# Layer 0's expert routing: all tiles at once behind the last norm, or four tiles at a time behind each group's norm

## The chip, the cores and the metric

The kernel runs on one core of one Trainium2 chip. The metric is the device time of one execution in microseconds (us); lower is better. Three runs of the kernel before took 4592.47, 4594.38 and 4607.38 us, so the median is 4594.38.

The engines are named as the profile names them: PE (TensorE, matrix products; PEld is its loading of weights), DVE (VectorE), ACT (ScalarE), POOL (GpSimd, which here issues the gathers and scatters whose rows are picked by an index) and SP (SyncE, which here issues plain copies).

## What is computed

Four layers of a graph network over 3125 nodes with 256 features and 50000 edges. Each layer adds a graph convolution and a mixer to x, then a feed-forward part with experts. The change touches layer 0 alone:

```python
xn = _layernorm(x)
x = x + _L0_gnn_ref(xn, src, dst, edge_type, ...) + _L0_mix_ref(xn, ...)
x = x + _L0_ffn_ref(_layernorm(x), ...)

# _L0_ffn_ref: each token goes to one of 8 experts, which take at most C = 489 tokens
probs = softmax(x @ gate_w + gate_b)
idx = argmax(probs)                      # the token's expert
prb = probs[idx]
one_hot = one_hot(idx, 8)
pos = (cumsum(one_hot, axis=0) * one_hot).sum(-1) - 1    # its place in the expert's list
kept = pos < C
buf = zeros(8, C, 256).at[idx, where(kept, pos, C)].set(x, mode='drop')
ybuf = relu(buf @ w1 + b1) @ w2 + b2     # per expert
y = ybuf[idx, minimum(pos, C - 1)] * (prb * kept)
```

The place pos is a running count over all tokens, so a token's row in buf depends on all tokens ahead of it, and on none behind it.

## The kernel before

The nodes lie in 25 tiles of 128 (T = 25, P = 128), which are handled in groups of four (GROUPS: six groups of four tiles and one of a single tile). The method fast() writes the whole run.

**Layer 0's first half** (lines 2384 to 2403) is a drive() of four generators that take turns: in each round seg_near makes three steps, l0_mix one, norm_after one, and sort_places two.
- seg_near (L434) is the graph convolution. The edges are sorted by destination and lie in 391 chunks of 128. Step i issues gather i on POOL (L447): 128 rows of a table in DRAM, picked by gi, go to one of 16 buffers G. The same step works off chunk i - 12: a one-hot of the destinations is made on DVE (L416) and multiplied on PE (L430, tile seg). When the last chunk of a tile is done, close (l0_close, L1027) adds the result to x and puts the tile on the list closed. Tile t closes with chunk 16t + 18.
- l0_mix (L1046) is the mixer. It puts a tile on the list mixed when it has been added to x.
- norm_after (L186) waits until the four tiles of a group are on both lists. Then it normalises them (norm_tiles, L170 to L181: statistics at L174 and L175, xn at L178, transposes on PE at L165) and calls then(t0, n), which before is gate0: sixteen small products with the gate's weights and an addition, which gives the group's scores pr (L1117).
- sort_places (L620) works out rows for a later sort of the edges by source.

**Behind the drive** the first 16 scatters of send (L687, table by_src) are issued on POOL. Then l0_ffn (L1121) does the experts. It clears the table moe_buf in DRAM with two copies from zeros (L1128 and L1130), takes the softmax of all 25 tiles' scores at once (L263 to L270), finds the first maximum (first_max, L219, with an iota made on POOL at L254), counts with two products against a triangle and against ones (L1140, L1142), sums over the tiles with one scan (L1151), and gets the rows wi for writing and ri for reading. Then 25 scatters on POOL (L357) send the tiles of xn to moe_buf. Eight experts follow: their rows are loaded (L1183), transposed (L1188) and multiplied. While they run, a Pump lets one by_src scatter of POOL go after every 700 columns of product. At the end 25 gathers on POOL (L351, yt) fetch each token's result, and the next norm follows.

**What sets the order.** A scheduling layer orders the instructions of PE, DVE, ACT and SP within a region when the program is built. POOL's are kept as the code issues them (manual_schedule for Pool around fast()). Each engine then works off its list, and semaphores make it wait for other engines' results. All plain copies of this part go through SP's queue.

Of the kernel before, what the change touches and what calls it, by code (L numbers as in the profile page):

```python
# [7 lines left out]
F32 = mybir.dt.float32  # L8
BF16 = mybir.dt.bfloat16
I32 = mybir.dt.int32  # L10
AF = mybir.ActivationFunctionType
OP = mybir.AluOpType
AX = mybir.AxisListType
# [4 lines left out]
P = 128  # L18
N = 3125
T = 25  # L20
NP = T * P
TAIL = N - (T - 1) * P
D = 256
# [11 lines left out]
CAP = 489  # L35
# [29 lines left out]
def drive(*gens):  # L65

    live = list(gens)
    while live:
        for g in list(live):
            for _ in range(g[1]):  # L70
                try:
                    next(g[0])
                except StopIteration:
                    live.remove(g)
                    break
# [19 lines left out]
class Net:  # L95
# [1022 lines left out]
                                 gb[:, None, :].to_broadcast([P, n, 8]))  # L1118
        return pr, gate

    def l0_ffn(self, pool, lean=False, pr=None):  # L1121
        nc, a = self.nc, self.a
        NE, FF = 8, 1024
        full = [P, T, NE]
        buf = self.dram.tile([NE * CAP, D], F32, name="moe_buf")
        ybuf = self.dram.tile([NE * CAP, D], F32, name="moe_y")
        flat = bass.AP(tensor=buf.tensor, offset=buf.offset, ap=[[NE * CAP * D // P, P], [D, 30], [1, D]])
        nc.sync.dma_start(flat, self.zeros[:, None, :].to_broadcast([P, 30, D]))  # L1128
        rest = NE * CAP * D // P - 30 * D
        nc.sync.dma_start(bass.AP(tensor=buf.tensor, offset=buf.offset + 30 * D,  # L1130
                                  ap=[[NE * CAP * D // P, P], [1, rest]]), self.zeros[:, :rest])
        if pr is None:
            pr, gate = self.l0_gate(pool)
            gate(0, T)
        self.softmax_last(pool, pr, full, "pr")
        iota = self.iota_e(pool, T, NE, "l0r")
        oh, prob, idx = self.first_max(pool, pr, full, iota, "l0r")
# [14 lines left out]
        pre = pool.tile(full, F32, name="pre")  # L1152
        nc.vector.tensor_add(pre, cum.rearrange("p e t -> p t e"), before.rearrange("p (t e) -> p t e", e=NE))
        nc.vector.tensor_mul(pre, pre, oh)
        pos = pool.tile([P, T], F32, name="pos")
# [3 lines left out]
        slot = pool.tile([P, T], F32, name="slot")  # L1159
        wi = pool.tile([P, T], I32, name="wi")  # L1160
        ri = pool.tile([P, T], I32, name="ri")
# [5 lines left out]
        nc.vector.tensor_mul(prob, prob, kept)  # L1167
        for t in range(T):
            self.scatter_apart(buf.name, buf, wi[:, t:t + 1], self.xn[:, t, :])
        inf = pool.tile([P, 4 * NE], F32, name="inf")  # L1170
        nc.vector.memset(inf, 0.0)
        b1 = self.load(pool, "b1", a["L0_ffn_b1"])
        mt = [(i * P, min(P, CAP - i * P)) for i in range(4)]
        for e in range(NE):
# [10 lines left out]
            for k in range(2):  # L1185
                p = self.ps(CAP)
# [4 lines left out]
            for f in range(FF // P):  # L1191
                p = self.ps(CAP)
# [3 lines left out]
            for i, (m0, m) in enumerate(mt):  # L1196
                p = self.ps(D, parts=m)
# [17 lines left out]
        p = self.ps(1)  # L1215
        nc.tensor.matmul(p, self.ones, fin, start=True, stop=True)
        nc.vector.tensor_scalar(ok, p, P - 0.5, None, op0=OP.is_gt)
        with self.tc.If(self.value(ok) > 0) as branch:
            for t0, n in GROUPS:
                for t in range(t0, t0 + n):  # L1220
                    y = self.gather(pool, "yt", ybuf, ri[:, t:t + 1], D, 4)
                    nc.vector.scalar_tensor_tensor(self.x[:, t, :], y, prob[:, t:t + 1], self.x[:, t, :],
                                                   op0=OP.mult, op1=OP.add)
# [1145 lines left out]
    def fast(self):  # L2369

        nc, tc, a = self.nc, self.tc, self.a
        g = self.g
        with tc.tile_pool(name="keepf", bufs=1) as keep, tc.tile_pool(name="dramf", bufs=1, space=DRAM) as dram:
# [7 lines left out]
            self.deg2 = keep.tile([P, T], F32, name="deg2")  # L2381
            ok4 = keep.tile([P, 1], I32, name="ok4")
            self.beyond = keep.tile([P, 1], F32, name="beyond")
            pr0, gate0 = self.l0_gate(keep)
            order = tp("order")
            op = order.__enter__()
            place = op.tile([P, C1], I32, name="place")
            rec = op.tile([P, C1, 3], F32, name="rec")
            with tp("gl0") as gp, Banks(self, **sums):
                gi = gp.tile([P, C1], I32, name="gi")  # L2390
                closed = set()
                with tp("set0") as sp:
                    ty = self.load(sp, "type", a["type"], dtype=I32)
                    nc.vector.scalar_tensor_tensor(gi, g["src"], 4.0, ty, op0=OP.mult, op1=OP.add)
                    nc.scalar.copy(rec[:, :, 2], self.load(sp, "weight", a["weight"]))
                    dst = self.load(sp, "dst", a["dst"], dtype=I32)
                    nc.scalar.copy(rec[:, :, 0], dst)
                    nc.scalar.copy(rec[:, :, 1], g["src"])
                with tp("mix0") as mp, tp("sort0") as sp:
                    skey = self.bits(sp, g["src"], "skey", 7)  # L2400
                    drive((self.seg_near(gp, g, self.h_tab, gi, self.l0_close(gp, closed), True), 3),
                          (self.l0_mix(mp), 1), (self.norm_after(closed, self.mixed, then=gate0), 1),
                          (self.sort_places(sp, skey, C1, T, self.sbase, place, 40), 2))
            with Banks(self, **plain):
                sorted_e = dram.tile([P * C1, 3], F32, name="by_src")
                send = self.send(sorted_e, place, rec, C1)
                for _ in range(16):
                    next(send)
                with tp("ffn0") as p:
                    self.pump = Pump(tc, send, 700)  # L2410
                    for _ in self.l0_ffn(p, True, pr0):
                        pass


            with tp("att1") as gp:
                closed, self.mixed = set(), set()
                pre = gp.tile([P, 4 * EG, 4], F32, name="pre")
# [353 lines left out]
```

## Time and profile before

| | us |
|---|---|
| median of three runs | 4594.38 |
| the profiled execution: its time | 4595.59 |
| its span on the core | 4593.9 |
| first gather of layer 0, last gather of layer 0 (start) | 147.2, 659.7 |
| scores of the seven groups, pr (start) | 420.7, 433.2, 451.0, 511.9, 591.8, 667.1, 685.0 |
| 25 scatters to moe_buf (start of the first and of the last) | 694.9, 725.8 |
| first load of the experts' rows, first product on them | 728.4, 730.4 |
| last gather of the experts' results (start) | 1008.6 |

The busiest engines over the span are PE with 3624.3 us and POOL with 2627.7. The profile is of one execution; a row of the timeline gives start and length in us, the engine, the line of the kernel, the operation, what it writes and reads, how many there are, and in brackets how long the engine was idle before it and what it waited for. The clock given is the one that PE was granted.

### The profile page before, as it was taken

Reading aid. Unit: us, or ns where it says so; the run is one execution under the profiler, and the core shown is the slowest. Engines: PE = TensorE matmul, PEld = TensorE weight load, DVE = VectorE, ACT = ScalarE, POOL = GpSimd, SP = SyncE. Lnnn points to the kernel's source line nnn. Section 1 sums busy time; section 2 is a strip of 40 time slices with the busy share of each in tenths; the row PEclk is TensorE's granted clock in tenths of the full one; section 3 lists DMA queues with packets and bytes.
Section 4 is the critical chain, followed back from the end, with each engine's and each line's share of the span. In section 5 each row is a group of like instructions: output and inputs, shape, how many; then the busy total and the mean of one; then the engine's idle time right before and its main releaser. Section 6 shows DMA issues by size and latency. Waiting matters only on the chain. (4 is left out here: it accounts for less than half of the span.)

```text
span 4593.9 us, 47098 instructions
## 1 busy us (share of the span) xinstructions
PE 3624.3 (79%) x13977; PEld 2408.6 (52%) x13977; DVE 2214.8 (48%) x7451; ACT 750.4 (16%) x1455; POOL 2627.7 (57%) x2605
## 2 busy tenths in 40 slices
PE   7889866945867867687787669998699995389898
PEld 3457544633544535455454434555466773257665
DVE  4477431145777875784545352113665233515443
ACT  2010001211100102113111011222122220012222
POOL 0577776755777747564777624770376565226550
PEclk9989877976988878788998878999898998588888
DMA  3433333314433320122333310001233234200000
GB/s 123 162 95 101 103 120 99 110 51 125 134 101 101 107 66 19 25 57 87 103 109 108 110 33 8 15 8 37 80 113 110 81 96 118 59 4 10 8 8 29
DMA packets 231200, 348.62 MB, mean 76 GB/s; under 512 B 74128, under 2 KB 168135, under 8 KB 230936
## 3 DMA queue, kind: packets, MB, share of 16 engines
q0 software_dynamic: 108384, 219.50, 17.2%
q1 hardware_dynamic: 118136, 121.97, 8.5%
q10 hardware_dynamic: 4416, 4.01, 0.3%
q8 instruction: 118, 1.93, 0.2%
q14 instruction: 146, 1.20, 0.1%
HBM read 294.62 MB, written 50.61 MB: 75 GB/s over the span
## 5 line engine op out<-in xcount | busy, mean ns | idle before, releaser
L430 PE MATMUL seg<-G,E 128*128 128x256 f32 (+1 forms) x3210 | 926.7, 421 | 206.3 <-DMA G<-tab,e3src 79.6
L430 PEld LDWEIGHTS seg<-G,E 128*128 128x128 f32 x3210 | 610.9, 205 | 490.7 <-issue 127.9
L110 PE MATMUL mm<-xnT,w 128*128 128x512 f32 (+1 forms) x1232 | 540.9, 585 | 21.0 <-DVE x L2200 20.7
L357 POOL DMA_INDIRECT by_src<-rec,place x391 | 431.2, 1103 | 186.4 <-PE mm L110 118.7
L416 DVE TENSOR_SCALAR E<-iota_row,e1dl 128x128 f32<-128x128 f32 (+1 forms) x1173 | 368.4, 324 | 348.8 <-PE seg L430 337.9
L447 POOL DMA_INDIRECT G<-h_tab,gi x391 | 385.8, 987 | 262.6 <-DMA selfw<-in_L_gnn_self_W 135.0
L842 POOL DMA_INDIRECT ring<-l1rows,e1src x391 | 428.7, 1096 | 131.9 <-issue 54.5
L447 POOL DMA_INDIRECT G<-tab,e1src x391 | 382.3, 978 | 203.6 <-PE seg L430 130.2
L447 POOL DMA_INDIRECT G<-tab,e3src x391 | 387.8, 992 | 123.2 <-PE seg L430 62.2
L430 PE MATMUL seg<-ring,E 128*128 128x264 f32 (+1 forms) x1762 | 423.0, 379 | 30.8 <-DVE E L416 21.9
L110 PE MATMUL mm<-w,hT 128*128 128x256 f32 (+1 forms) x1712 | 398.8, 385 | 0.5 <-ACT hT L1550 0.5
L357 POOL DMA_INDIRECT by_dst<-rec,place x256 | 251.6, 983 | 233.8 <-PE mm L110 188.7
L842 POOL DMA_INDIRECT ring<-l3rows,e2src x256 | 248.2, 970 | 225.1 <-PE seg L430 156.1
L430 PEld LDWEIGHTS seg<-ring,E 128*128 128x128 f32 x1762 | 307.0, 212 | 117.4 <-DVE E L416 50.3
L110 PEld LDWEIGHTS mm<-xnT,w 128*128 128x128 f32 x1232 | 235.9, 205 | 243.9 <-issue 213.2
L110 PEld LDWEIGHTS mm<-w,hT 128*128 128x128 f32 (+1 forms) x1712 | 317.8, 190 | 59.1 <-issue 16.9
L165 PE MATMUL mm<-ident,xn 128*128 128x128 f32 x400 | 94.7, 393 | 227.3 <-DVE xn L178 223.8
L418 DVE TENSOR_SCALAR E<-iota_row,e3dl,rec 128x128 f32<-128x128 f32 (+1 forms) x391 | 144.4, 383 | 221.4 <-PE seg L430 220.0
L1710 DVE SCALAR_TENSOR_TENSOR x<-mm,l2t_r,x 128x256 f32<-128x256 f32 x150 | 70.8, 483 | 300.6 <-PE mm L110 300.6
L165 PEld LDWEIGHTS mm<-ident,xn 128*128 128x128 f32 x400 | 66.0, 192 | 257.0 <-DVE xn L178 175.0
L854 DVE TENSOR_TENSOR ring<-ring,ex 128x260 f32<-128x260 f32 (+1 forms) x647 | 193.4, 322 | 2.5 <-ACT ex L834 2.3
L1703 ACT ACTIVATE h<-mm,b 128x512 f32<-128x512 f32 (+1 forms) x168 | 107.2, 641 | 360.1 <-PE mm L110 359.9
(710 smaller groups left out, 4976.8 us busy)
## 6 DMA issues: line engine op xcount, KB each, us to landing
w<-in_L_ffn_w SPq DMA_DIRECT2D x16, 1024.0 KB
h_tab<-htab_s SPq DMA_DIRECT2D x25, 512.0 KB
r_b<-rowa SPq DMA_DIRECT2D x64, 128.0 KB
bn_h<-c_h SPq DMA_DIRECT2D x50, 128.0 KB
G<-h_tab,gi POOLq DMA_INDIRECT x391
by_src<-rec,place POOLq DMA_INDIRECT x391
ring<-l1rows,e1src POOLq DMA_INDIRECT x391
G<-tab,e3src POOLq DMA_INDIRECT x391
```

The source lines that it names most:

```text
L110: m = self.nc.tensor.matmul(out, l, r, start=(i == 0), stop=(i == last))
L165: self.nc.tensor.transpose(p[:, i * P:(i + 1) * P], src(t0 + i)[:, k * P:(k + 1) * P], self.ident)
L357: return self.nc.gpsimd.indirect_dma_start(out=table, out_offset=bass.IndirectOffsetOnAxis(ap=idx, axis=0), in_=src, in_offset=None, bound ...
L416: self.nc.vector.tensor_scalar(e[:, :w], self.iota2[:, :w], g["dl"][:, c:c + 1], None, op0=OP.is_equal)
L418: self.nc.vector.tensor_scalar(e[:, :w], self.iota2[:, :w], g["dl"][:, c:c + 1], weight[:, c:c + 1], op0=OP.is_equal, op1=OP.mult)
L430: self.nc.tensor.matmul(A[t], e, rows_c, start=first, stop=last)
L447: nc.gpsimd.indirect_dma_start(out=ring[i % len(ring)][:, :D], out_offset=None, in_=table, in_offset=bass.IndirectOffsetOnAxis(ap=gidx[:, ...
L842: nc.gpsimd.indirect_dma_start(out=ring[:, i % RING].rearrange("p h f -> p (h f)"), out_offset=None, in_=table, in_offset=bass.IndirectOff ...
L854: nc.vector.tensor_mul(r[:, :, :d + 1], r[:, :, :d + 1], ex[:, c, :, None].to_broadcast([P, 4, d + 1]))
L1703: nc.scalar.activation(o[:, f, :n], p, AF.Relu, bias=b[:, 2 * e + f:2 * e + f + 1])
L1710: nc.vector.scalar_tensor_tensor(self.x[:, t, :], p, r[:, t, e:e + 1], self.x[:, t, :], op0=OP.mult, op1=OP.add)
```

## The change

l0_ffn is cut in three. l0_buffer clears moe_buf. l0_route gives a function step(t0, n), which norm_after now calls in place of gate0: it works out one group's gate, softmax, expert, count and rows, and issues the group's scatters at once. The counts of the groups before are kept in run, one column of eight totals per tile. The old way for all tiles stays as l0_route_all for the other path of the program (general()), which isn't taken here. l0_route is called at the head of fast(), so moe_buf is cleared there; the small tiles move from one pool to another.

```diff
-    def l0_ffn(self, pool, lean=False, pr=None):
+    def l0_buffer(self):
...
+    def l0_route(self, pool):
+        nc, NE, G = self.nc, 8, 4
+        buf = self.l0_buffer()
+        pr, gate = self.l0_gate(pool)
+        iota = self.iota_e(pool, G, NE, "l0r")
+        run = pool.tile([P, T + 1, NE], F32, name="l0_run")
...
+        nc.vector.memset(run[:, 0, :], 0.0)
+
+        def step(t0, n):
+            gate(t0, n)
...
+            nc.vector.tensor_reduce(m, s, axis=AX.X, op=OP.max)
+            nc.vector.tensor_sub(s, s, mb)
+            nc.scalar.activation(s, s, AF.Exp)
+            nc.vector.tensor_reduce(m, s, axis=AX.X, op=OP.add)
+            nc.vector.reciprocal(m, m)
+            nc.vector.tensor_mul(s, s, mb)
+            nc.vector.tensor_reduce(prob[:, tl], s, axis=AX.X, op=OP.max)
+            nc.vector.tensor_tensor(oh, s, prob[:, tl, None].to_broadcast(full), op=OP.is_lt)
+            nc.vector.scalar_tensor_tensor(oh, oh, float(NE), iota[:, :n], op0=OP.mult, op1=OP.add)
+            nc.vector.tensor_reduce(idx, oh, axis=AX.X, op=OP.min)
+            nc.vector.tensor_tensor(oh, iota[:, :n], idx[:, :, None].to_broadcast(full), op=OP.is_equal)
+            p = self.ps(2 * n * NE)
+            for j, w in enumerate((self.triu, self.ones)):
+                nc.tensor.matmul(p[:, j * n * NE:(j + 1) * n * NE], w, oh.rearrange("p t e -> p (t e)"),
+                                 start=True, stop=True)
+            pv = p.rearrange("p (j t e) -> p j t e", j=2, e=NE)
+            for i in range(n):
+                nc.vector.tensor_add(run[:, t0 + i + 1, :], run[:, t0 + i, :], pv[:, 1, i, :])
+            nc.vector.tensor_add(pre, run[:, tl], pv[:, 0])
+            nc.vector.tensor_mul(pre, pre, oh)
+            nc.vector.tensor_reduce(pos, pre, axis=AX.X, op=OP.add)
+            nc.vector.tensor_scalar(m, pos, float(CAP), None, op0=OP.is_lt)
+            nc.vector.tensor_scalar(slot, m, 1.0, -8192.0, op0=OP.subtract, op1=OP.mult)
+            nc.vector.tensor_add(slot, slot, pos)
+            nc.vector.scalar_tensor_tensor(wi[:, tl], idx, float(CAP), slot, op0=OP.mult, op1=OP.add)
+            nc.vector.tensor_scalar(slot, pos, float(CAP - 1), None, op0=OP.min)
+            nc.vector.scalar_tensor_tensor(ri[:, tl], idx, float(CAP), slot, op0=OP.mult, op1=OP.add)
+            nc.vector.tensor_mul(prob[:, tl], prob[:, tl], m)
+            for t in range(t0, t0 + n):
+                self.scatter_apart(buf.name, buf, wi[:, t:t + 1], self.xn[:, t, :])
+        return (buf, ri, prob), step
...
+    def l0_ffn(self, pool, routed=None):
...
+        lean = routed is not None
+        buf, ri, prob = routed or self.l0_route_all(pool)
...
-            pr0, gate0 = self.l0_gate(keep)
             order = tp("order")
             op = order.__enter__()
+            routed, route0 = self.l0_route(op)
...
-                          (self.l0_mix(mp), 1), (self.norm_after(closed, self.mixed, then=gate0), 1),
+                          (self.l0_mix(mp), 1), (self.norm_after(closed, self.mixed, then=route0), 1),
...
-                    for _ in self.l0_ffn(p, True, pr0):
+                    for _ in self.l0_ffn(p, routed):
```

More of the change, by code (lines that the diff above doesn't have):

```diff
@@ L1119, in l0_gate @@
         return pr, gate
-    def l0_ffn(self, pool, lean=False, pr=None):
-        nc, a = self.nc, self.a
-        NE, FF = 8, 1024
-        full = [P, T, NE]
+    def l0_buffer(self):
+        nc, NE = self.nc, 8
         buf = self.dram.tile([NE * CAP, D], F32, name="moe_buf")
-        ybuf = self.dram.tile([NE * CAP, D], F32, name="moe_y")
         flat = bass.AP(tensor=buf.tensor, offset=buf.offset, ap=[[NE * CAP * D // P, P], [D, 30], [1, D]])
@@ L1131, in l0_ffn @@
                                   ap=[[NE * CAP * D // P, P], [1, rest]]), self.zeros[:, :rest])
-        if pr is None:
-            pr, gate = self.l0_gate(pool)
-            gate(0, T)
+        return buf
+    def l0_route(self, pool):
[4 more added lines that the diff above has]
+        run = pool.tile([P, T + 1, NE], F32, name="l0_run")
+        prob = pool.tile([P, T], F32, name="l0_prob")
+        wi = pool.tile([P, T], I32, name="l0_wi")
+        ri = pool.tile([P, T], I32, name="l0_ri")
+        nc.vector.memset(run[:, 0, :], 0.0)
+        def step(t0, n):
+            gate(t0, n)
+            tl = slice(t0, t0 + n)
+            t2 = lambda nm: pool.tile([P, G], F32, name="l0_" + nm, bufs=2)[:, :n]
+            t3 = lambda nm: pool.tile([P, G, NE], F32, name="l0_" + nm, bufs=2)[:, :n]
+            full = [P, n, NE]
+            s, m, idx, oh, pre, pos, slot = pr[:, tl], t2("m"), t2("idx"), t3("oh"), t3("pre"), t2("pos"), t2("slot")
+            mb = m[:, :, None].to_broadcast(full)
+            nc.vector.tensor_reduce(m, s, axis=AX.X, op=OP.max)
[29 more added lines that the diff above has]
+        return (buf, ri, prob), step
@@ L1135, in l0_ffn, with l0_route_all @@
+    def l0_route_all(self, pool):
+        nc, NE = self.nc, 8
+        full = [P, T, NE]
+        buf = self.l0_buffer()
+        pr, gate = self.l0_gate(pool)
+        gate(0, T)
         self.softmax_last(pool, pr, full, "pr")
@@ L1169, in l0_ffn @@
             self.scatter_apart(buf.name, buf, wi[:, t:t + 1], self.xn[:, t, :])
+        return buf, ri, prob
+    def l0_ffn(self, pool, routed=None):
+        nc, a = self.nc, self.a
+        NE, FF = 8, 1024
+        full = [P, T, NE]
+        ybuf = self.dram.tile([NE * CAP, D], F32, name="moe_y")
+        lean = routed is not None
+        buf, ri, prob = routed or self.l0_route_all(pool)
         inf = pool.tile([P, 4 * NE], F32, name="inf")
```

## The prediction, made before the changed kernel was run

> **What bounds the kernel now.** I read the busy slices first, then the stretch from 140 to 1010 us, where all that the change touches lies, in the table of windows and in POOL's and DVE's timelines; and beside them the order in which the two built programs put the instructions on each engine.
>
> ```profile
> PE 3624.3 (79%) x13977; PEld 2408.6 (52%) x13977; DVE 2214.8 (48%) x7451; ACT 750.4 (16%) x1455; POOL 2627.7 (57%) x2605
> ```
>
> PE is the busiest engine over the span, but that mean hides the stage. Windows (columns: PE, PEld, DVE, ACT, POOL busy us and instructions, granted clock, DMA share, GB/s):
>
> ```profile
> 500.00:560.00 60.00, 46.98 (x168) 32.30 (x168) 21.95 (x75) 1.36 (x5) 45.67 (x48) 0.89 0.36 105
> 660.00:685.00 25.00, 7.79 (x40) 5.51 (x40) 7.09 (x26) 2.48 (x6) 16.81 (x18) 0.65 0.60 191
> 700.00:730.00 30.00, 0.00 (x0) 0.00 (x0) 0.00 (x0) 0.00 (x0) 20.66 (x21) 0.50 0.28 101
> 800.00:900.00 100.00, 98.78 (x367) 66.41 (x366) 13.74 (x45) 21.05 (x32) 76.24 (x78) 1.00 0.36 111
> ```
>
> POOL stands at 0.76 in each full stretch. That is its ceiling: a gather is 0.95 busy and 0.30 ahead of the next, 0.95/1.25 = 0.76; a scatter takes 0.98 + 0.30 (1.29 from start to start). POOL's timeline:
>
> ```profile
> 659.66 0.95 POOL L447 DMA_INDIRECT G<-h_tab,gi  x1 [0.30 <-PE seg L430]
> 660.91 1.02 POOL L357 DMA_INDIRECT by_src<-rec,place  x1 [0.30 <-issue]
> ...
> 681.28 0.41 POOL L254 IOTA l0r_ii<- 128x200 int32 x1
> 694.88 0.99 POOL L357 DMA_INDIRECT moe_buf<-xn,wi  x1 [13.19 <-DVE slot L1165]
> ...
> 725.83 0.98 POOL L357 DMA_INDIRECT moe_buf<-xn,wi  x1 [0.30 <-issue]
> 737.15 0.98 POOL L357 DMA_INDIRECT by_src<-rec,place  x1 [10.34 <-PE mm L110]
> ...
> 973.69 0.98 POOL L357 DMA_INDIRECT by_src<-rec,place  x1 [0.30 <-issue]
> 974.98 0.99 POOL L351 DMA_INDIRECT yt<-moe_y,ri  x1 [0.30 <-issue]
> ```
>
> So POOL is the chain of layer 0: 391 gathers, 16 by_src scatters, 25 moe_buf scatters, about 184 pumped by_src scatters, then the y gathers, which follow without a gap although PE's expert products ended at 962.6. PE's emptiness from 667 to 730 costs less than it seems. The change adds no POOL instruction and takes none away but the size of an iota; it only moves them. **What it is worth is the change in POOL's idle time between 147 and 975 us.**
>
> **Idle that goes.** 13.2 us ahead of the first moe_buf scatter, 10.3 + 0.65 + 1.1 us until the first pumped scatters got their products: 25.3, because the 16 by_src scatters now stand behind the last moe_buf scatter and fill that hole. The iota, 0.4 + 0.3, moves to the start, where POOL is idle. POOL's small waits for PE behind gather 198 (5.7 us over the 1.25 of each) vanish if POOL gets late for other reasons. Together -31.7.
>
> **Idle that comes: the scatters in the gather queue.** POOL's rows stand in the order of the built program, one instruction holding up the next. In the changed program the four scatters of a group stand behind gather 197, 209, 221, 272, 335 and 390 (counted from 0), the last one behind those. Each waits for the group's row numbers (wi); behind it wait all later gathers, and for those PE. Two rows show how late wi is:
>
> ```profile
> 411.11 0.94 POOL L447 DMA_INDIRECT G<-h_tab,gi  x1 [0.30 <-PE seg L430]
> ...
> 420.66 0.19 DVE L1117 TENSOR_TENSOR pr<-mm,rb_L_ffn_gate_b 128x32 f32<-128x32 f32 x1 [1.25 <-PE mm L110]
> ...
> 654.67 0.94 POOL L447 DMA_INDIRECT G<-h_tab,gi  x1 [0.30 <-PE seg L430]
> 658.26 0.16 ACT L1034 COPY deg<-seg 128x1 f32<-128x1 f32 x1 [19.93 <-PE seg L430]
> 667.06 0.19 DVE L1117 TENSOR_TENSOR pr<-mm,rb_L_ffn_gate_b 128x32 f32<-128x32 f32 x1 [1.65 <-PE mm L110]
> ```
>
> The row at 411.11 is gather 197: POOL is free at 412.4, but the first group's gate scores come at 420.7. The row at 654.67 is gather 386: its product is over at 658.3, so 3.6 us lie between a gather's start and the end of its product.
> The route has no row at this size. Its nearest rows: dependent DVE steps on 128x25 at 693.77, 693.98, 694.20 come 0.21 apart, on 128x200 0.40 apart; I take 0.21, since the tiles are 128x32 and 128x4. Gate scores to one-hot: ten DVE steps and an exp on ACT (0.4 with its waits), and hand-overs, 3.5. The two counting products (L1140 and L1142 take 1.8 for 200 columns from one-hot to copy): 0.7. Products to wi: eleven steps and a little, 2.5.
> The built program puts these two products behind the very chunk of the last gather ahead of the scatters (197, 221, 272, 335; for the second group 208). So even with all else ready, POOL waits 3.6 + 0.7 + 2.5 - 1.25 = 5.5.
> Group 1: scores 420.7; DVE's order has some 18 other instructions (sort scans, one-hots, x updates) between them and the one-hot, 6.3 in all; 0.9; then 5.0 to wi, for the same reason: 432.9, a wait of 20.6.
> Group 2: gather 198 at 438.2, chunk 208 done at 454.3, wi 460.4; POOL is free at 453.2: 7.2.
> Group 3: gather 210 at 465.6; gate behind chunk 216, wi 489.2, POOL free at 480.6: 8.6.
> Group 4: no sort any more. The gate stands behind chunk 269, three gathers (3.75) before the last: 3.6 - 3.75 + gate 2.0 + 0.2 + 3.5 + 0.7 + 2.5 - 1.25 = 7.5. Group 5: behind 333, two before: 8.8.
> Sum 52.7 (between 36, dependent steps alone and 5.5 for the later groups, and 80, with steps of 0.40).
>
> **The tail.** Nothing covers it any more, since the 16 by_src scatters went behind it. From the last gather's start: gate scores of group 6 end 7.6 later (667.25 - 659.66), route 3.5 + 0.7 + 2.5, three updates of tile 24 between (0.8): 15.1, POOL idle 13.9. Four scatters, to 20.3. Tile 24: its norm and gate 3.3 (681.91 to 685.20), its route 5.2, done at 24.7: idle 4.4. Sum 18.3 (16 to 24).
>
> **The start.** moe_buf's zeros, 3840 KB, were issued behind type and selfw:
>
> ```profile
> 142.07 0.43 SPq L123 DMA_DIRECT2D type<-in_type  x1
> ...
> 145.04 0.43 SPq L1128 DMA_DIRECT2D moe_buf<-zeros  x1
> 145.59 0.57 DVE L2394 SCALAR_TENSOR_TENSOR gi<-e1src,type 128x391 int32<-128x391 int32 x1 [1.65 <-DMA type<-in_type]
> 147.20 1.10 POOL L447 DMA_INDIRECT G<-h_tab,gi  x1 [135.00 <-DMA selfw<-in_L_gnn_self_W]
> ```
>
> Now they stand ahead on SP, and no gather starts before type is there. At the 350 GB/s that the windows show from 150 to 165 they take 11 us, so gathers may start up to 10 later. But POOL lost 11 us to a full ring by gather 84, while PE ran the mixer's products at full: PE hardly moves, and these waits shrink instead. I take +2, between 0 and +10. The Trainium skill ("DMA: Bandwidth & Descriptors", Queues, rings and completion order) says that a DMA engine takes the descriptors of a ring in order, which would make the full 11 us come; no run here shows yet whether a small load passes. By that rule without any cover the sum would be 8 more.
>
> **At nothing.** DVE's extra work: some 25 steps a group, hidden in its idle time (22 of 60 us busy in the first window) but for what is counted above. The running sums, 28 tiny adds: in the 2.5. ACT's Exp and Sqrt now alternate, 1.28 a table load in the row at 684.12; it ran while the scores were made, and so it stands here. The Trainium skill ("ScalarE: Activation LUTs", What ACT_TABLE_LOAD costs) puts a switch at about 2.66 us with its drain; seven on the path would be 19 us more. Scores wait for two products behind the copy that precedes the load, so I leave it at nothing.
>
> **Sum:** 52.7 + 18.3 + 2 - 31.7 = +41.3. The profiled execution took 4595.6 (span 4593.9), 1.2 above the median of 4594.4: 4637. Later stages keep their order in the built program and are only shifted.
>
> **Rivals.**
> *POOL never waits in the gather queue.* Place: the five groups before the tail. A group closes 12 chunks ahead of the gather POOL is at, 15 us of cover; if wi is there when POOL comes, the 52.7 are 0: -11.4, 4584, and with a tail half as long 4575. It decides as soon as the counting products run five chunks earlier than the built order has them; that order, and 420.7 against 412.4, speak against it.
> *POOL is not what ends the expert stage.* PE's first product would come at 764 in place of 730 (last gather 734.5, plus 24.7, 1.0, and the 3.5 from 726.8 to 730.35): +33, 4629. Against it: the pump ended ten us behind PE, and now begins later still.
> *The zeros delay the gathers in full:* +8, 4645.
> *The scatters wait as long as the upper bounds say:* 4664.
>
> **How the numbers follow.** Forecast 0.60; PE ends the stage 0.10; zeros in full 0.13; upper bounds 0.07; POOL never waits 0.10. Range: from the lower bounds (36 + 16 + 0 - 31.7 = +20; 4616, and a little lower for slips in both) to the upper ones: 4610 to 4664. Repeated measurements of this kernel can tell 0.3%, 14 us. Only the never-waits case can end below 4609: faster 0.04, same 0.07, slower 0.89.
>
> **What would show it.** POOL idle ahead of moe_buf scatters, five blocks of 7 to 21 us between 412 and 740 and two in the tail; moe_buf scatters of one group 1.29 apart; the first expert product near 764; no POOL gap before the pump; y gathers near 1016. Wrong would be: gathers that go on at 1.25 across a group's scatters; a first gather far behind 157.

## The result, and the profile after

The changed kernel takes 4648.72 us (median of four runs, 4645.90 to 4661.87) against 4593.43 of the kernel before (median of four, 4582.92 to 4607.38): a ratio of 1.0125, with a 95% interval of 1.0108 to 1.0141. It is slower by 55 us; the prediction said 41. Some of the experiments ran on other chips, on which the kernel before takes 5116 and 5076 us; only ratios, and times of one chip, are compared below. The ratios come from all runs of both kernels, beside each other on one chip, so that with scattered runs one can differ from the quotient of the two medians (most in e3 below: 1.0101, and 1.0064 by the medians).

The profiled execution of the changed kernel took 4661.87 us (span 4660.1), the highest of its four. The busy times of its whole span hardly differ from those before:

```profile
PE 3664.1 (79%) x14001; PEld 2426.6 (52%) x14001; DVE 2229.5 (48%) x7592; ACT 766.6 (16%) x1473; POOL 2625.9 (56%) x2605
```

POOL has the same 2605 instructions and almost the same busy time (2627.7 before). The windows of the changed kernel (columns as before), the first as it was shown of before, the second around the last gather, which has moved:

```profile
500.00:560.00 60.00, 44.38 (x160) 29.41 (x160) 26.25 (x84) 2.06 (x5) 45.68 (x48) 0.94 0.36 103
740.00:770.00 30.00, 15.81 (x70) 11.73 (x69) 15.07 (x73) 7.33 (x12) 9.09 (x10) 0.73 0.37 117
```

Where no scatter of a group falls (500 to 560), POOL issues its 48 instructions as before. At the end of the gathers (740 to 770) it issues 10 in 30 us, although before, in the emptiest stretch, it issued 21. POOL's timeline of the changed kernel shows where its time went (the number in brackets is its idle time ahead of the row):

```profile
412.52 0.94 POOL L447 DMA_INDIRECT G<-h_tab,gi  x1 [0.30 <-PE seg L430]
435.14 1.02 POOL L357 DMA_INDIRECT moe_buf<-xn,l_wi  x1 [21.67 <-DVE ln_mv L175]
...
463.20 1.02 POOL L357 DMA_INDIRECT moe_buf<-xn,l_wi  x1 [6.65 <-DVE l_wi L1177]
...
495.62 1.02 POOL L357 DMA_INDIRECT moe_buf<-xn,l_wi  x1 [11.11 <-DVE l_wi L1177]
...
575.51 1.02 POOL L357 DMA_INDIRECT moe_buf<-xn,l_wi  x1 [10.36 <-DVE l_slot L1178]
...
671.18 1.02 POOL L357 DMA_INDIRECT moe_buf<-xn,l_wi  x1 [11.14 <-DVE l_slot L1178]
...
744.44 0.94 POOL L447 DMA_INDIRECT G<-h_tab,gi  x1 [0.30 <-PE mm L110]
760.34 1.02 POOL L357 DMA_INDIRECT moe_buf<-xn,l_wi  x1 [14.95 <-DVE l_wi L1177]
...
769.12 0.98 POOL L357 DMA_INDIRECT moe_buf<-xn,l_wi  x1 [3.83 <-DVE l_slot L1178]
770.41 0.98 POOL L357 DMA_INDIRECT by_src<-rec,place  x1 [0.30 <-issue]
...
1026.23 0.98 POOL L357 DMA_INDIRECT by_src<-rec,place  x1 [0.30 <-issue]
1027.52 0.99 POOL L351 DMA_INDIRECT yt<-moe_y,l_ri  x1 [0.30 <-issue]
```

Seven blocks, one ahead of each group's first scatter. The releaser named is the DVE row that ended last: l_slot of L1178 and ln_mv of L175 stand just behind wi of L1177 on DVE, so all seven are waits for the group's row numbers. Behind 770.41 POOL has no gap to the first gather of the results, which starts at 1027.52 in place of 974.98: +52.5. PE's last expert product ends at 1009.5, 18 us earlier. So POOL still ends the expert stage, and the loss is complete there; the first rows of layer 1 are +52.7 late, and the medians differ by 55.3. The end of the profiled execution is later still by some 13 us; layer 2's scatters by destination, of which the first starts 54.5 late and the last 62.4 late, carry most of that. The median of the four runs lies 13 us below this execution, so these 13 us aren't shown as a cost of the change.

### The profile page after: what moved, and what is told of

It is laid out like the page before. It is cut to its first block, busy times and chain, and to the rows that moved or that the text cites. A ratio compares the mean times of both kernels' runs of the same rounds, so it can differ in the third digit from the quotient of the medians.

```text
span 4660.1 us, 47250 instructions
## 1 busy us (share of the span) xinstructions
PE 3664.1 (79%) x14001; PEld 2426.6 (52%) x14001; DVE 2229.5 (48%) x7592; ACT 766.6 (16%) x1473; POOL 2625.9 (56%) x2605
## 5 line engine op out<-in xcount | busy, mean ns | idle before, releaser
L430 PE MATMUL seg<-G,E 128*128 128x256 f32 (+1 forms) x3210 | 944.7, 426 | 255.3 <-DMA G<-tab,e3src 79.3
L416 DVE TENSOR_SCALAR E<-iota_row,e1dl 128x128 f32<-128x128 f32 (+1 forms) x1173 | 366.8, 322 | 393.1 <-PE seg L430 382.2
```

Source lines behind the costliest of these rows:

```text
L416: self.nc.vector.tensor_scalar(e[:, :w], self.iota2[:, :w], g["dl"][:, c:c + 1], None, op0=OP.is_equal)
L430: self.nc.tensor.matmul(A[t], e, rows_c, start=first, stop=last)
```

## The experiments

In none of them is a part of the computation left out. The theory is that of the prediction: POOL works off its list in order, a group's four scatters stand ahead of gathers that are ready, and their wait for wi is what the change costs. The rivals: scatters cost the gathers something by themselves, or the tail behind the last gather is the larger part, or the zeros at the start are, or PE and not POOL ends the stage.

### The wait in the gather queue, and the tail: four kernels on one chip

These four ran on one chip, on which the kernel before takes 4600.99 us. They cross two edits. **Held**: the scatters of groups 1 to 5 are issued eight rounds of the drive later (24 gathers: behind gather 221, 233, 245, 296 and 359 in place of 197, 209, 221, 272 and 335), when wi is there. The route is still called where the change calls it, but in the built order its counting products come 3, 10, 16, 2 and 3 chunks later too. **Filled**: behind the last gather POOL gets 11 by_src scatters, then group 6's scatters, 3 more, group 7's, 2 more, in place of the two groups and then 16.

```diff
         def step(t0, n):
+            self.waiting.append([t0, n, 0])
             gate(t0, n)
...
+        def out(t0, n):
             for t in range(t0, t0 + n):
                 self.scatter_apart(buf.name, buf, wi[:, t:t + 1], self.xn[:, t, :])
+        self.out_rows = out
...
+    def l0_out(self, hold, groups):
+        sent = 0
+        while sent < groups:
+            for w in self.waiting:
+                w[2] += 1
+            if self.waiting and self.waiting[0][2] > hold:
+                self.out_rows(*self.waiting.pop(0)[:2])
+                sent += 1
+            yield
...
-                          (self.sort_places(sp, skey, C1, T, self.sbase, place, 40), 2))
+                          (self.sort_places(sp, skey, C1, T, self.sbase, place, 40), 2), (self.l0_out(8, 5), 1))
...
-                for _ in range(16):
-                    next(send)
+                for k in (11, 3, 2):
+                    for _ in range(k):
+                        next(send)
+                    if self.waiting:
+                        self.out_rows(*self.waiting.pop(0)[:2])
```

e11 is this diff. e9 has l0_out(0, 5), so that the scatters stand where the change has them, and the filled tail. e8 has l0_out(8, 5) and sends the two waiting groups and then the 16, as the change does. e10 is the changed kernel.

> The changed kernel itself, on the chip of e8, e9 and e11: ratio near 1.0125 by all theories; on a chip where gathers land late, waits of 7 to 30 us ahead of each group as in e4.

> Scatters of the first five groups held back by eight rounds, tail as in the changed kernel (group 6, tile 24, then 16 by_src). Theory: the stage waits (61 us on POOL in the changed kernel's profile) are gone, the tail's 19 stay: ratio to before near 0.997, 1.5% below the changed kernel. Rival (the exposed tail is what the change costs): near the changed kernel's 1.012.

> The changed kernel with only the tail filled (11 by_src scatters, group 6, 3 by_src, tile 24, 2 by_src), scatters not held back. Theory: the stage waits stay; the tail gives back at most 11 us where POOL ends the expert stage, and next to nothing where PE does: ratio 1.009 to 1.012. Rival (the tail is the cost): 1.000 or below.

> The kernel of e2 and e6, on the chip of e8, e9 and e10. Theory: ratio 0.996 to 0.998, at or just below e8. Rival (tail filling is what makes it fast): well below e8, by 0.4% or more.

| | held | filled | us | ratio to before, 95% | idle ahead of scatters of groups 1 to 5 | first gather of results |
|---|---|---|---|---|---|---|
| e10 | no | no | 4649.80 | 1.0101 (1.0086 to 1.0117) | 22.0, 8.6, 13.3, 10.1, 11.0 | 1032.8 |
| e9 | no | yes | 4651.90 | 1.0102 (1.0087 to 1.0118) | 21.3, 8.6, 13.3, 9.8, 10.8 | 1027.5 |
| e8 | yes | no | 4594.48 | 0.9986 (0.9977 to 0.9995) | none over 1 | 971.0 |
| e11 | yes | yes | 4591.35 | 0.9973 (0.9963 to 0.9984) | none over 1 | 963.4 |

Holding the scatters is worth 55 us with the bare tail and 61 with the filled one: the whole loss (48.8 us on this chip), and a little. POOL's timeline of e8, at group 1 and behind the last gather:

```profile
443.15 0.95 POOL L447 DMA_INDIRECT G<-h_tab,gi  x1 [0.30 <-PE seg L430]
444.40 1.06 POOL L357 DMA_INDIRECT moe_buf<-xn,l_wi  x1 [0.30 <-DVE l_oh L1164]
...
448.37 0.99 POOL L357 DMA_INDIRECT moe_buf<-xn,l_wi  x1 [0.30 <-issue]
449.66 1.00 POOL L447 DMA_INDIRECT G<-h_tab,gi  x1 [0.30 <-issue]
...
686.26 0.95 POOL L447 DMA_INDIRECT G<-h_tab,gi  x1 [0.30 <-PE seg L430]
703.89 1.02 POOL L357 DMA_INDIRECT moe_buf<-xn,l_wi  x1 [16.69 <-DVE l_wi L1180]
```

The four scatters sit among the gathers and take 5.26 us (444.40 to 449.66), with no gap on either side. e8's last gather is 26.6 us later than in the first profile of before (of another chip); 20 scatters of 1.29 are 25.8, and 0.8 is left. So scatters among gathers cost what they take themselves, and that is taken off again behind the last gather. With the waits the whole loss is gone; that the counting products come later as well can't be the reason, since it makes wi later and not earlier. That e8 still has its tail of 16.69 + 3.83 and yet ends no later than before puts the tail in second place.

The filled tail of e11:

```profile
699.50 0.98 POOL L357 DMA_INDIRECT by_src<-rec,place  x1 [0.30 <-issue]
702.86 0.98 POOL L357 DMA_INDIRECT moe_buf<-xn,l_wi  x1 [2.37 <-DVE l_wi L1180]
...
711.97 0.98 POOL L357 DMA_INDIRECT moe_buf<-xn,l_wi  x1 [0.30 <-DVE l_ri L1182]
...
726.79 0.98 POOL L357 DMA_INDIRECT by_src<-rec,place  x1 [10.50 <-PE mm L110]
```

The 16 by_src scatters cover all of the tail's wait but 2.37 us, but then there are none left for the time in which the experts' first rows are loaded and multiplied: POOL stands idle for 10.50 us there, waiting for the pump. What the tail gives, the pump takes back, all but some 5 to 8 us of the first gather of the results (e9 against e10 5.3, e11 against e8 7.6). In the times, e9 is 2 us above e10 and e11 3 us below e8, with intervals that overlap: filling the tail isn't shown to be worth anything by itself. e11 beats both kernels: 0.9973 of the one before.

### Holding by two rounds only

The same edit with l0_out(2, 7), and the tail as the change has it. This one ran on a chip on which the kernel before takes 5116.17 us.

> As the changed kernel, but each group's scatters are issued two rounds (6 gathers, 7.5 us) later. Theory: each wait shrinks by what the six gathers cover, unless the built order puts the counting products later too (it does: behind chunk 200, 214, 225, 274, 341 against last gathers 203, 215, 227, 278, 341): group 1 near 14, 2 near 5, 3 near 5, 4 near 1, 5 near 6, sum 31 against the 61 of the changed kernel; tail as in the changed kernel; time near 4620. Rival (the waits are set by the length of the route alone, or by DVE's load, whatever stands ahead on POOL): sum still near 60, time near 4648.

It took 5149.07: 1.0101 (1.0067 to 1.0134). The waits ahead of groups 1 to 5 are 20.9, 16.2, 11.3, 13.9 and 13.4, together 75.6, where 31 were expected. The 61 that they were expected to shrink from were of another chip, though. On this one the kernel of e4 (below), which doesn't hold its scatters, waits 29.6, 12.4, 13.9, 19.8 and 17.1, together 92.7. Beside it two rounds took 17 us off (8.7, -3.8, 2.6, 5.9 and 3.7), although two rounds are six gathers, 7.5 us of POOL, for each of the five groups. The time shows nothing of it: 1.0101 and 1.0102, with intervals that overlap.

One reason stands in the built order: the counting products moved too. They stand behind chunks 200, 214, 225, 274 and 341, where the changed kernel has them behind 197, 208, 221, 272 and 335. The scatters stand behind gathers 203, 215, 227, 278 and 341, so the distance from counting product to scatter has become 3, 1, 2, 4 and 0 chunks, all under the five from which the prediction's rival was to decide; in e8 and e11 (products behind 200, 218, 237, 274 and 338) it is 21, 15, 8, 22 and 21. Whether that is all of it, no run shows. What is shown is that two rounds left most of the wait on this chip, and that eight took it away on the chip of e8 and e11; nothing between was run.

### All scatters behind the drive, and held scatters, on the slower chips

e1 issues all 25 scatters behind the 16 by_src scatters, as the kernel before does, but keeps the route in groups. e2 and e6 are the kernel of e11.

```diff
+        def out(t0, n):
             for t in range(t0, t0 + n):
                 self.scatter_apart(buf.name, buf, wi[:, t:t + 1], self.xn[:, t, :])
+        self.out_rows = out
...
                 for _ in range(16):
                     next(send)
+                self.out_rows(0, T)
```

> Routing per group as in the changed kernel, but all 25 moe_buf scatters stand behind the 16 by_src scatters, as before. Theory (only POOL's waits in the gather queue and the exposed tail cost time): gathers go on at 1.25 us, last gather near 661, first moe_buf scatter near 683 without a wait (before 694.9 after 13.2 us of waiting), y gathers near 963, time 4582 (about -12 against before). Rival (the extra DVE and PE work per group, the table loads, or the zeros at the head cost it): the time stays above before, 4600 to 4648, and gathers come late without any moe_buf scatter among them.

> The scatters of the first five groups are held back by eight rounds of the drive (24 gathers), and the tail is filled: 11 by_src scatters, the four of group 6, 3 by_src, the one of tile 24, 2 by_src. Theory: no wait ahead of any moe_buf scatter but a few us, last gather near 685, first expert product near 714, y gathers near 957, time 4575. Rival (a scatter among gathers costs in itself, through the queue or the DMA engines): gathers slower than 1.25 us behind each group, time at or above before.

> The kernel of e2 again, to have it beside another run of before: on a chip where a gather lands within 3.6 us (as in the first profile) the theory gives 18 us less than before (ratio 0.996), y gathers near 957. Rival (scatters among gathers cost in themselves): ratio at 1.000 or above.

e1: 5109.13, 0.9994 (0.9974 to 1.0014). Its scatters start at 785.0, and the first 20 have no wait; but group 6's stand behind a wait of 12.2 us and tile 24's behind one of 5.3. So the route in groups doesn't take away the 13.2 us that before waits ahead of all 25; a wait of about that length now stands further back. The time shows no gain and no loss, and its interval still holds the 12 us that were expected (0.9977). e2: 5103.70, 0.9979 (0.9958 to 1.0001); e6, beside 5076.13: 5052.53, 0.9959 (0.9942 to 0.9977). The absolute times expected were for the first chip and missed; the ratios agree with e11's 0.9973. The waits didn't vanish as far as they did in e11: 3.5 and 1.9 us are left ahead of groups 2 and 3 in e2, 7.4 and 2.8 in e6, and 18.5 and 19.9 ahead of group 6, where a few were expected. Still, on both kinds of chip the loss lies in where the scatters stand, and not in the route.

Something of why these chips are slower can be seen in the same stretch of time, though not at the same work, since in e7 the mixer and the sort are still at work there. The gathers' group of lines, from 500 to 560 us, of the kernel before in its first profile (busy us and mean ns, then idle time ahead and what ended it):

```profile
L447 POOL DMA_INDIRECT G<-h_tab,gi x48 | 45.9, 956 | 14.6 <-PE seg L430 9.5 <-issue 4.3 <-PE mm L165 0.3
```

and of the same kernel on the slower chip (e7, below):

```profile
L447 POOL DMA_INDIRECT G<-h_tab,gi x36 | 36.7, 1020 | 23.5 <-PE seg L430 14.5 <-issue 5.8 <-remote 2.5
```

36 gathers in place of 48 in the same 60 us, and 23.5 us idle. POOL waits there for PE to free the buffers, so in this stretch it isn't the chain. Why PE is later isn't shown: the mean granted clock of PE over the span is 0.811 there and 0.858 in the first profile, 5 to 6% less, but the time is 10 to 11% longer.

### The zeros at the start

The two copies that clear moe_buf are issued behind type, weight and dst, instead of ahead of all of them.

```diff
-        return self.l0_clear(buf)
+        self.l0_zero.append(buf)
+        return buf
...
                     dst = self.load(sp, "dst", a["dst"], dtype=I32)
...
+                    self.l0_clear(self.l0_zero[0])
```

> The changed kernel with the two copies of zeros behind type, weight and dst on SP's queue. Theory: first gather back near 147 (156 in the changed kernel), but gather 100 only 1 to 2 us earlier, since PE's full ring takes the rest; time within 3 of the changed kernel's 4648. Rival (the start passes through to the end): 9 earlier, 4639.

It took 5160.33 beside 5116.17: 1.0102 (1.0072 to 1.0132). The changed kernel itself wasn't run on this chip; the nearest kernel beside it is e3, with the zeros ahead and the scatters two rounds later, at 1.0101. So there is no gain to be seen. The first gather starts at 146.18 in place of the 155.2 of e3, 9.0 earlier. Gather 34 is still 9.9 earlier (193.98, 203.85), but gather 50 is 2.1 later (229.78, 227.66), and gather 100 1.3 earlier (303.10, 304.42). The nine microseconds are absorbed within 50 gathers.

### by_src behind the scatters, in the kernel before

The one part of the change that the route isn't needed for: the 16 by_src scatters go behind the 25 to moe_buf. e7 is the kernel before, for its profile on that chip.

```diff
         for t in range(T):
             self.scatter_apart(buf.name, buf, wi[:, t:t + 1], self.xn[:, t, :])
+        if self.pump is not None:
+            for _ in range(16):
+                next(self.pump.gen)
...
-                for _ in range(16):
-                    next(send)
```

> The kernel before, with one edit: the 16 by_src scatters stand behind the 25 moe_buf scatters instead of ahead of them. Theory (POOL's work between the first gather and the y gathers sets the end, not PE's start on the experts): the experts' first product comes about 12 us earlier, near 718, but the y gathers start within 3 us of before (973 against 975), and the time is the same within 0.2%. Rival (PE's start sets the end of the stage): y gathers near 963, time 12 us shorter (0.26%).

> The kernel before, unchanged: gives the profile of before on this chip, against which the POOL timelines of the others of this call are read. All theories: the time of before.

e5 took 5072.00 beside 5076.13: 0.9987 (0.9964 to 1.0010), nothing that can be told from no change, as the theory had it. Its first expert product is 29 us earlier than in e7 (806.2, 835.1), but the first gather of the results only 11 (1104.5, 1115.4), and of that the time shows 4, with an interval from 18 faster to 5 slower. That gather is the rival's mark (12 earlier) and not the theory's (within 3); but e5's last gather of layer 0 is already 3.2 earlier than e7's (744.1, 747.2), where the edit changes nothing, and each is a single profile. A start 29 us earlier on PE is mostly lost again before the stage ends. This chip was the slower one, so it settles nothing for the first, where the trace of the changed kernel shows POOL without a gap up to the first gather of the results.

## Why the prediction was right, and where its sizes were off

The sign, the place and the mechanism were right. Measured on the two first profiles, between the first gather and the first gather of the results (waits less the ordinary 0.30 ahead of each instruction, as the prediction counts them):

| term | forecast | measured |
|---|---|---|
| waits of groups 1 to 5 | 52.7 | 59.4 |
| tail | 18.3 | 18.2 |
| idle of before that is gone | -25.3 | -24.1 |
| iota | -0.7 | -0.4 |
| gathers from 198 on, over their ordinary time | -5.7 | -3.9 |
| start | +2 | +1.4 |
| moe_buf's scatters themselves (26.7 busy, 24.6 before) | 0 | +2.1 |
| by_src's scatters themselves | 0 | -0.2 |
| sum | +41.3 | +52.5 |

The sum is what the first gather of the results was late by.

**The waits of groups 1 to 5** are the step that was mis-sized: 20.6, 7.2, 8.6, 7.5 and 8.8 were forecast, 21.4, 6.4, 10.8, 10.1 and 10.8 measured. The first two hold within 0.9; groups 3 to 5 are each two to three short, 6.8 together. Group 4 shows what was short in 4 and 5. Timeline of the changed kernel, PE, DVE and POOL in order of time:

```profile
563.04 1.91 PE L165 MATMUL mm<-ident,xn 128*128 128x128 f32 x8
564.21 0.95 POOL L447 DMA_INDIRECT G<-h_tab,gi  x1 [0.30 <-PE mm L165]
564.75 1.90 PE L430 MATMUL seg<-G,E 128*128 128x257 f32 x4
566.46 1.87 PE L110 MATMUL mm<-gw,xnT 128*128 128x8 f32 x16
568.37 0.19 DVE L1117 TENSOR_TENSOR pr<-mm,rb_L_ffn_gate_b 128x32 f32<-128x32 f32 x1 [1.40 <-PE mm L110]
572.16 0.19 DVE L1163 TENSOR_TENSOR l_oh<-l0r_if,l_idx 128x32 f32<-128x32 f32 x1
572.50 0.38 PE L1166 MATMUL mm<-l_oh,triu 128*128 128x32 f32 x2 [1.47 <-DVE l_oh L1163]
575.07 0.16 DVE L1177 SCALAR_TENSOR_TENSOR l_wi<-l_idx,l_slot 128x4 int32<-128x4 f32 x1
575.51 1.02 POOL L357 DMA_INDIRECT moe_buf<-xn,l_wi  x1 [10.36 <-DVE l_slot L1178]
```

From the end of the scores (568.56) to the scatter it takes 6.95 us; 3.5 + 0.7 + 2.5 = 6.7 were forecast. The steps on DVE come 0.22 apart for the most part, as taken from the nearest rows. But the scores end 4.35 us behind the start of the last gather, and 2.05 were forecast (3.6 - 3.75 + 2.0 + 0.2). The gate stands behind chunk 269 in the built order, as the prediction read it. What was mis-sized is the 3.6 us from a gather to the end of its product, which came from the row of gather 386, where PE waits for data. Chunk 269's gather starts at 560.47 and its product ends at 566.65, 6.2 us later. PE has work here almost without a pause from 557.1 on, and its granted clock is low just then. Windows of the changed kernel around the gates of groups 4 and 5:

```profile
557.00:567.00 10.00, 9.73 (x28) 6.33 (x28) 4.00 (x12) 1.87 (x2) 6.33 (x7) 0.53 0.36 107
652.00:662.00 10.00, 9.66 (x23) 5.71 (x24) 4.06 (x12) 0.82 (x2) 6.21 (x7) 0.50 0.37 106
```

and of e8 around the same chunk 269:

```profile
521.00:531.00 10.00, 7.92 (x45) 6.36 (x46) 4.82 (x16) 2.10 (x3) 7.56 (x9) 1.00 0.36 105
```

At a clock of 0.53 the products of one chunk take 0.63 to 0.77 us in place of 0.38; in e8, at 1.00, chunk 269's product ends 4.0 us behind the start of its gather (523.47 to 527.51), while e8's own chunk 333, at 0.52 to 0.60, has 6.9. In group 5 chunk 333's ends 5.9 us behind, at 0.50, and the scores end 5.3 behind the last gather's start, where 3.3 were forecast: that is the whole of its miss. The rows of before could have told it: there chunk 269's product ends 7.1 us behind its gather's start, at a clock of 0.56. Why the clock falls in these stretches no run shows.

Group 3 missed for another reason. Its gate isn't late: chunk 216's lag is 3.5 us, and the scores end at 482.11, 13.0 behind gather 210 (469.14). But from there to the scatter (495.62) it takes 13.5 us, since DVE's order has one-hots (L416) and updates of x (L1102) between the steps of the route, which themselves wait up to 1.8 us for PE.

**The two counting products** do not set the wait of group 4 then: the one-hot is ready at 572.35, and PE takes them at 572.50. The floor of 5.5 us that the prediction put under each group by their place in the order held (the smallest wait is 6.4).

**The rest of the miss** of 11.2 us is the scatters themselves, 2.1 us longer than before (several of a group's four are slower than 0.98), the gathers behind 198 with 1.8, 1.2 of old idle time, in which the forecast left the ordinary 0.30 of four instructions, and smaller pieces that nearly cancel.

**The gathers behind 198** came near their forecast by luck. The 5.7 us were read as waits for PE that vanish when POOL is late. But POOL's idle time ahead of these gathers is the ordinary 0.30 but for 0.9 us in all; the excess of before is eleven gathers that ran 1.05 to 2.89 us in place of 0.95. The changed kernel still has nine longer ones (1.06 to 1.53). Why some run longer no run shows.

**The 13.2 us of before** have a second reason that the prediction didn't read. DVE's timeline before, behind the last gather (659.66):

```profile
669.22 0.43 DVE L174 BATCH_NORM_STATS2 ln_st<-x 128x6 f32<-128x256 f32 x1
681.73 0.27 DVE L255 CAST l0r_if<-l0r_ii 128x200 f32<-128x200 int32 x1 [12.08 <-DMA by_src<-rec,place]
681.91 0.17 DVE L175 BATCH_NORM_AGGREGATE ln_mv<-ln_st 128x2 f32<-128x6 f32 x1
```

DVE stands for 12.08 us ahead of the cast of the iota, which POOL issues only behind the 16 by_src scatters (681.28), and tile 24's norm stands behind that cast in DVE's order, although its statistics are ready at 669.65. By these rows some 12 of the 13.2 us (an estimate) are the price of the iota's place. The change makes its iota at the start, and the forecast booked that at 0.7. The iota alone wasn't moved in any run, so what that small edit would have given stays open.

**The tail** came as forecast, 14.65 and 3.53 less the ordinary 0.30, where 13.9 and 4.4 were forecast.

**The start** came as forecast in its size. Timeline of SP, DVE and POOL in the changed kernel:

```profile
141.10 8.02 SPq L1128 DMA_DIRECT2D moe_buf<-zeros  x1
...
151.80 0.89 SPq L123 DMA_DIRECT2D type<-in_type  x1
...
155.33 0.57 DVE L2460 SCALAR_TENSOR_TENSOR gi<-e1src,type 128x391 int32<-128x391 int32 x1 [4.51 <-DMA type<-in_type]
...
156.18 1.11 POOL L447 DMA_INDIRECT G<-h_tab,gi  x1 [13.86 <-DVE gi L2460]
```

The first gather is 9.0 later than before, and the waits for full buffers that followed before shrink by 7.4: gather 84 is 1.6 later, gather 197 1.4. (The prediction has POOL lose 11 us by gather 84 before; its rows give 10.0.) The rival of the zeros that delay in full is out, by this and by e4. The way of it was another, though. From its issue to gi, type takes 3.5 us here (151.80 to 155.33), and 3.5 before (142.07 to 145.59). The delay lies ahead of that, on SP, which stands for 8.02 us in the issue of the second copy of the zeros. The Trainium skill ("DMA: Bandwidth & Descriptors", Queues, rings and completion order) says that a DMA engine takes the descriptors of a ring in order. This trace neither confirms nor refutes it: at the 350 GB/s of the prediction the 3840 KB, issued at 140.68, take until about 152 (an estimate), and type was issued at 151.80, when they were nearly through.

**ACT's table loads**, taken at nothing, cost nothing. In the tail, the tightest place, the timeline of ACT in the changed kernel has

```profile
762.97 1.28 ACT L1155 ACT_TABLE_LOAD   x1
764.54 0.21 ACT L1155 ACTIVATE pr<-pr 128x8 f32<-128x8 f32 x1 [0.29 <-DVE pr L1154]
```

The copy ahead of the load ends at 762.96, the load is over at 764.25, and the exp waits 0.29 for DVE; in all seven groups the exp waits for DVE behind its load. The Trainium skill ("ScalarE: Activation LUTs", What ACT_TABLE_LOAD costs) has about 2.66 us for a switch with its drain, which from 762.97 would last until 765.6. The exp starts at 764.54, so the trace has 1.28 for the load here and no drain on top of it, and the measurement decides.

**The rivals.** POOL never waits: not so in the changed kernel, but e8 and e11 are that case made on purpose, and they give -6.5 us (e8, with the tail bare), where -11.4 was worked out, and -9.6 (e11, with it filled), where 4575 would be some -19. The prediction's mark for it, counting products five chunks ahead of where the built order has them against POOL, isn't contradicted: with 8 to 22 chunks no wait over 1 us is left on that chip (on the slower ones, in e2 and e6, up to 7.4), and with 0 to 4 every group waits. PE ends the stage: not on the first chip, where POOL has no gap and PE ends 18 us earlier. Its first expert product came at 779.0, not at 764: 10 us of that are the last gather, which was later than forecast, and the other 5 lie between the last scatter and the first load of the experts' rows (725.83 to 728.39 before, 769.12 to 775.50 here). Upper bounds: 80 for the five groups; 59.4 came.

What stays open: why e3's waits were as long as they were, why the granted clock falls where the gates of groups 4 and 5 stand, and the 13 us by which the first profile of the changed kernel ends later than the stage explains.

## What to carry to other kernels

A scatter put into a queue that works in order costs its own 1.29 us if its indices are there when the queue reaches it, and otherwise all of the wait, for everything behind it. So when work is moved forward, count from the queue's position to the moment at which the last operand is ready, and issue it that much later: the same scatters 24 gathers later turned 1.0101 into 0.9986. And take the lag between a load and its product from a row in which the consumer is as busy, and its granted clock as low, as it will be at that place: 3.6 us were taken here, 6.2 came.

## What the runs showed of the hardware that was not expected

SP's issue of a copy can take 8.0 us: the second copy of the zeros did so in the changed kernel (8.01 to 8.03 in the profiles of e2, e8, e9, e10 and e11). In e4 it is the same copy, again, behind type:

```profile
141.76 0.43 SPq L124 DMA_DIRECT2D type<-in_type  x1
...
144.25 8.80 SPq L1136 DMA_DIRECT2D moe_buf<-zeros  x1
```

That second copy is only 72 KB; what stands ahead of it is the one of 3840 KB. In the kernel before it took 0.33 us (162.27), and the long one was the copy that SP issued next behind the 3840 KB there, of 256 KB:

```profile
147.41 7.33 SPq L1049 DMA_DIRECT2D wkv<-in_L_mix_W_qk  x1
```

So in these three kernels it is the next issue behind the large copy that is long, 7.3 to 8.8 us. What stands behind that on SP is held with it; what stands ahead of the large copy (type, in e4 and before) isn't. What SP waits for there the traces don't name.

The same kernel took 4594 to 4601 us on one chip, or two like it, and 5076 and 5116 on others, 10 to 11% more, at a granted clock of 0.81 to 0.82 in place of 0.85 to 0.86. Between 500 and 560 us POOL waits for PE there (23.5 us ahead of its gathers), and the edits that shorten POOL's chain at the start (e4) or behind the gathers (e5) didn't show in the time.
